# Layer 1's first convolution done in halves twice, with the projection ahead of it: two attention blocks on one core

## The chip, the cores and the metric

The kernel runs on one core of a Trainium2 chip. The metric is device time in microseconds (us), the median of three runs. A core has a tensor engine (PE; its weight loads are listed apart as PEld), VectorE (DVE), ScalarE (ACT), GpSimd (POOL), and a sync engine (SP) that mostly issues transfers (DMA). Each engine works through its own list of instructions in order; semaphores connect the lists.

## The reference, cut to what matters

Eight images of 512 channels and 32 x 32 pixels (1024 tokens) go through two attention blocks, one after the other, all in fp32:

```python
# layer 0: 32 groups, 8 heads of 64 channels
h = group_norm(x); q, k, v = split(w_qkv @ h + b_qkv)
x = x + w_proj @ (softmax(q.T k / 8) applied to v) + b_proj
# layer 1: 8 groups, one head of 512 channels
h = group_norm(x); q, k, v = q_w @ h + q_b, k_w @ h + k_b, v_w @ h + v_b
x = x + p_w @ (softmax(q.T k / sqrt(512)) applied to v) + p_b
```

All convolutions are 1 x 1, so each is a product of a 512 x 512 matrix and a 512 x 1024 image.

## The kernel before, in words

**Algebra.** In layer 1 the query and key weights are multiplied once, in a prologue, into one matrix M, and the value and output weights into Z. Layer 1 is then: g = M h (plus a bias), scores from g and h, z = Z h, and the product of the exponentials with z. So a sample has seven large stages: in layer 0 `v`, `k`, `q`, the attention of 8 heads, the projection `p`; in layer 1 `g` ("layer 1's first convolution"), the scores, `z`, the product with z.

**Halving.** Every product outside the heads is done by Winograd's form of Strassen's rule (`wino`, L227): both factors are cut in 2 x 2 blocks, sums of blocks are formed ("factors", `left_sums` L151 and `right_sums` L165), and 7 block products take the place of 8. The seven are issued in the order 1, four of `middle`, then 4 and 3; products 1, 2 share PSUM bank pair a, 6, 7, 4 pair b, 5, 3 pair c, and VectorE and ScalarE take the sums out in `done`. The last two products and what follows them are put on a list (`tail`) and issued only after the next stage's first product (`finish`), so that PE has work while the next stage's inputs become ready. `conv2` (L416) does so twice for `k` and `q`: each of the 7 products of half size is again done by 7 of quarter size, 49 matmuls of 256 columns for one convolution. For it GpSimd forms the inner factors of the image (`inner_factors`, L400: four subtractions for each of the 7 outer products), and the doubly cut weights are made once in the prologue by `keep2` (L296) and kept in DRAM.

**Order over the samples.** Layer 1 of sample b - 1 runs after the attention of sample b. One turn of the loop (L928) is: attention of sample b (eight stretches, one for each pair of heads `hp` and half of the tokens `tb`: 8 score tiles, exponentials, 8 products with v, sums, inverse); `g` of sample b - 1; projection of b; scores, z and the product with z of b - 1; `v`, `k`, `q` of b + 1. For b = 0 it is attention, `v` of sample 1, projection, `k`, `q`.

**What sets the order.** Matmuls are pinned in program order (L67). On the other engines a planner orders instructions when the kernel is built: each is placed when its inputs are expected to be ready and its buffer is free, earlier ones in the program first, so that a ready instruction may go ahead of one that stands before it; one wrapped in `tc.keep_in_program_order` ("pinned") stays behind the instruction traced just before it on its engine. Small VectorE work is queued on `background` and emitted a few pieces after each product (`run_background`), or all at once (`all_background`). `hooks` are lists of functions, one list after each product (after each pair of products in `conv2`). In attention, `extra[2 s]` is run after the scores of stretch s and `extra[2 s + 1]` after its products with v.

**Buffers.** 32 SBUF tiles of 4 KB a partition are shared by all images, factors and exponentials (`big`). Weights go through a ring of three buffers (`wpool`, 14 KB a partition each); `uses` lists the weights in order of use, and `load_weight` (L317) fetches the next one when a buffer has been read to the end. The PSUM pools are made anew for each kind of stage (`psum_pools`).

**The end of an attention stretch.** `reciprocals` (L548): PE sums the exponentials over partitions (`sums`), VectorE inverts them (L559), GpSimd keeps a running check sum (`all_recs`, L561), and the inverse goes to DRAM and back, spread over partitions (L563, L573). GpSimd then multiplies `a` (L615); in the last stretch VectorE does it later, in `scaled` (L617).

**Statistics of layer 1.** The projection's `residual` adds bias and x (L845, L847) and queues the statistics of each half (`half_stats`, L98; `end_stats`, L103) on `background`. `norm_hooks` (L861) are handed to the scores: `all_background` after the third product of the scores' first half, `group_mean` (a matmul and four small VectorE operations) after the fourth, `affine` (a matmul, then GpSimd's power) after the fifth.

**Weights for M.** The prologue's `later` prepares p, m and z during the first stretches of attention 0: three buffers of the ring, four subtractions each, a transfer to DRAM (`keep`), and after each the load of the next weight in use.

Of the kernel before, what the change touches and what calls it, by code (L numbers as in the profile page):

```python
# [29 lines left out]
def two_attention_blocks_kernel(  # L30
# [145 lines left out]
    def main_path(ctx):  # L176
# [116 lines left out]

        wdram2 = {n: dram.tile([P, 7, 7, P], F32, name=f"sums2_{n}") for n in "qk"}

        def keep2(n, t):  # L296

            u = wpool.tile([P, 4, 7, P], F32, tag="w", name=f"prepare2_{n}")
            quarter = lambda k, i: t[:, :, k, ts(i, P)]
            a11, a21, a12, a22 = quarter(0, 0), quarter(0, 1), quarter(1, 0), quarter(1, 1)  # L300
            s1, s2, s3, s4 = (u[:, i, :, :] for i in range(4))
            for dst, x, y, op in (
                (s1, a21, a22, ALU.add), (s2, s1, a11, ALU.subtract), (s3, a11, a21, ALU.subtract),
                (s4, a12, s2, ALU.subtract),
            ):
                nc.gpsimd.tensor_tensor(dst, x, y, op)
            for j, f in enumerate((a11, a12, s4, a22, s1, s2, s3)):
                nc.sync.dma_start(wdram2[n][:, :, j, :], f)

        twice = [("k", 0), ("k", 1), ("q", 0), ("q", 1)]  # L310
        uses = ["v", "p", *twice] if B > 1 else ["p"]
        for b in range(1, B):
            uses += ["m", "p", "z"] + (["v", *twice] if b + 1 < B else [])
        uses += ["m", "z"]
        loaded = []

        def load_weight():  # L317
            if uses:
                n = uses.pop(0)
                t = wpool.tile([P, 7 * C], F32, tag="w", name=f"w_{n[0]}_{len(uses)}")  # L320
                if n in twice:
                    t = t.rearrange("p (i j m) -> p i j m", i=4, j=7)
# [16 lines left out]

        def image_factors(h, uid):  # L340

            tiles = [pair_tile(f"t{i}_{uid}") for i in (1, 2, 4)]
            halves = lambda t: (t[:, :HT], t[:, HT:])
            return right_sums(
                [halves(t) for t in h[:2]], [halves(t) for t in h[2:]],
                [lambda j, t=t: t[:, j, :] for t in tiles], nc.vector.tensor_sub,
            )
# [51 lines left out]

        def inner_factors(hf, uid):  # L400

            f, steps = {}, []
            for p in ORDER:
# [5 lines left out]
                def make(ops=((t1, b12, b11), (t2, b22, t1), (t3, b22, b12), (t4, b21, t2))):  # L409
                    for dst, x, y in ops:  # L410
                        nc.gpsimd.tensor_tensor(dst, x, y, ALU.subtract)

                steps.append(make)
            return f, steps

        def conv2(n, f, bias, name, hooks=(), late=None):  # L416

# [121 lines left out]
            pair(2, (7,), [(1, 0)], [(0, 1)], [lambda: biased_half(1, 1)])  # L539
            last = [lambda: biased_half(0, 1), lambda: biased_half(1, 0)]  # L540
            if late is not None:
                late += last
                last = []
            pair(3, (3, 4), [(0, 1), (1, 0)], [(0, 1), (1, 0)], [load_weight, *last])
            return out


        def reciprocals(total, uid, across):  # L548

# [12 lines left out]
            rows = rowpool.tile([2, 4, P], F32, tag="rows", name=f"rows_{uid}")  # L562
            nc.sync.dma_start(rows.rearrange("j i n -> i j n"), rc[0:P:32, :, :])  # L563
            if across:
                r = pair_tile(f"r_{uid}")
                for j in range(2):
                    row = rows[j : j + 1].rearrange("j i n -> j (i n)")
                    nc.sync.dma_start(r[:, j, :], row.to_broadcast([P, HT]))
            else:
                r = rpool.tile([P, HT], F32, tag="r", name=f"r_{uid}")  # L570
                for j in range(2):
                    row = rows[j : j + 1].rearrange("j i n -> j (i n)")
                    nc.sync.dma_start(r[ts(j, 64), :], row.to_broadcast([64, HT]))  # L573
            return r


        def attention0(b, q, k, v, extra):
            a = channel_tiles(f"a0_{b}")
            n = 0
            for hp in range(KC):  # L580
                for tb in range(2):
                    uid = f"0_{b}_{hp}_{tb}"
# [29 lines left out]
                    nc.scalar.copy(dst, av)  # L612
                    r = reciprocals(total, uid, False)
                    if (hp, tb) != (KC - 1, 1):
                        nc.gpsimd.tensor_tensor(dst, dst, r, ALU.mult)  # L615
                    else:
                        scaled = lambda dst=dst, r=r: nc.vector.tensor_mul(dst, dst, r)  # L617

            assert not extra
            return a, scaled  # L620


        def scores1(b, gf, hf, uid, hooks):
# [7 lines left out]
            def part(j):  # L631
# [33 lines left out]

                wino(f"sc_{uid}_{j}", mm, done, middle=(6, 2, 5, 7) if j else (2, 5, 6, 7), hooks=() if j else hooks)

# [84 lines left out]
        def prologue():  # L752
# [44 lines left out]
            later = []  # L797
            for n in "pmz":
                t, steps = prepare(n)
                later.append(steps)  # L800
                later.append([lambda n=n, t=t: keep(n, t), load_weight])
            later.append([
# [3 lines left out]
            ])  # L806
            return v, q, k, norm1, later

        psum_pools("first", 2)
        v, q, k, norm0, later = prologue()  # L810

# [21 lines left out]

        def attention_steps(a, scaled, b):
            af, steps = image_factors(a, f"a_{b}")
            return af, [[], [scaled, lambda: background.extend(steps)]]

        def projection(b, af, xt):

            norm = GroupNorm(1, f"1_{b}")  # L840

            def residual(i, r, c, ps, u):
                oc = 2 * r + i
                xh = xt[oc][:, ts(c, HT)]
                nc.vector.scalar_tensor_tensor(xh, ps, obias[0][:, oc : oc + 1], xh, ALU.add, ALU.add)  # L845
                if u is not None:
                    nc.vector.tensor_add(xh, xh, u)  # L847
                background.append(lambda: norm.half_stats(oc, c, xh))

                if c == 1 - r:  # L850
                    background.append(lambda: norm.end_stats(oc))

# [4 lines left out]

            by_channel(weight("p"), af, f"p_{b}", residual, after=[load_weight, store])
            return norm

        def norm_hooks(norm, uid):  # L861
            return [
                [], [], [all_background], [lambda: norm.group_mean(acc_tile(f"gmean_{uid}")[:, :KC])],
                [lambda: norm.affine(acc_tile(f"gvar_{uid}")[:, :KC])],
            ]

        def values(b, h, hooks=()):

            hf, steps = image_factors(h, f"h0_{b}")
            background.extend(steps)  # L870
            inner, steps = inner_factors(hf, f"h0_{b}")
# [19 lines left out]

        def layer1_scores(b, h, hooks):
            hf, steps = image_factors(h, f"h1_{b}")
            background.extend(steps)
            g = conv(
                weight("m"), hf, ubias, f"g1_{b}", middle=(2, 5, 6, 7), hooks=hooks, back=4,
                after=[load_weight, lambda: background.extend(gsteps)],
            )
            stiles = [pair_tile(f"sg{i}_{b}") for i in (1, 2, 4)]
# [4 lines left out]
            )  # L904
            return hf, gf

        def layer1_rest(b, hf, gf, hooks, ahead):
            e, total, ef = scores1(b, gf, hf, f"1_{b}", hooks)
            state = {}
# [18 lines left out]
        for b in range(B):  # L928
# [11 lines left out]
            for i, f in enumerate(applies):  # L940
                extra[2 * i + 3].append(f)
            if b > 0:
                extra[0] += late
            psum_pools(f"attention_{b}", 1)
            a, scaled = attention0(b, q, k, v, extra)
            psum_pools(f"products_{b}", 2)
            xt = [load_x(b, c, "x") for c in range(KC)]
            af, ends = attention_steps(a, scaled, b)
            if b > 0:
                hf, gf = layer1_scores(b - 1, h, ends)  # L950
                norm1 = projection(b, af, xt)
                if b + 1 < B:
# [3 lines left out]
                ahead = [loads, *([f] for f in applies)]  # L956
                layer1_rest(b - 1, hf, gf, norm_hooks(norm1, f"1_{b}"), ahead)
                if b + 1 < B:
                    v, f, norm0 = values(b + 1, h)
                    q, k, late = keys_and_queries(b + 1, f, norm0, ())  # L960
            elif B > 1:
                v, f, norm0 = values(1, h, ends)
                norm1 = projection(0, af, xt)
                q, k, late = keys_and_queries(1, f, norm0, norm_hooks(norm1, "1_0")[1:])
            else:
                for f in sum(ends, []):
                    f()
                all_background()
                norm1 = projection(0, af, xt)
                finish()  # L970
                for f in sum(norm_hooks(norm1, "1_0"), []):
                    f()
                h, loads, applies = begun(load_again, norm1, 0, "h1")
                for f in loads + applies:
                    f()
        hf, gf = layer1_scores(B - 1, h, ())
        layer1_rest(B - 1, hf, gf, (), ())
        finish()

# [194 lines left out]
```

## Time and profile before

| | |
|---|---|
| time, median of 3 (lowest, highest) | 2905.97 us (2902.11, 2907.01) |
| profiled execution | 2900.9 us, granted clock 0.999 |
| one attention stretch | 14.65 us (418.17 to 432.83) |
| one turn of the loop, sample 1 to sample 2 | 355.16 us (330.10 to 685.26) |

One turn of the loop by stage, from the trace (start of the attention of sample 1 at 330.1 us):

| stage | from, to (us) | PE busy | DVE busy | POOL busy |
|---|---|---|---|---|
| `g` and most of the projection | 447.5 to 488.8 | 41.3 | 30.1 | 1.0 |
| scores and start of z | 488.8 to 537.3 | 48.5 | 27.8 | 3.2 |
| last attention stretch | 432.8 to 447.5 | 14.65 | 13.1 | 3.0 |

How to read it: busy times are the sums of the instructions' durations in the window. A matmul in fp32 is two records of the trace, each with a weight load of its own. The end of a matmul in the profile is modelled, and a record's duration overlaps with the next, so speed is read from the distance between starts. An engine that is idle while PE works costs nothing by itself. Lines in the profile name the helper (L67 for all matmuls, L238 for sums in PSUM), so stages are told apart by the names of the tiles.

### The profile page before, as it was taken

To read this page: it belongs to the slowest core of one execution; us is meant where nothing else is said; L and a number is where in the kernel's file an instruction comes from. 1 tells how busy PE (TensorE), PEld (TensorE's weight loads), DVE (VectorE), ACT (ScalarE), POOL (GpSimd) and SP (SyncE) were. 2 spreads that over 40 slices of the span, in tenths; PEclk is the share of its full clock that TensorE was granted. 3 is DMA by queue.
4 is the path that set the end of the run, shared out by engine and by line. 5 is a ranking of instruction groups with operands and counts; after the bars stand their busy time and mean duration, and the time that the engine had idled before them with its cause. 6 is when DMAs were issued, how large, how long until landed. Compare 5 with 4: busy or idle time off the path is not lost.

```text
span 2900.9 us, 29024 instructions
## 1 busy us (share of the span) xinstructions
PE 2886.5 (100%) x10838; PEld 1500.3 (52%) x10838; DVE 1932.5 (67%) x2613; ACT 872.2 (30%) x1117; POOL 468.9 (16%) x525
## 2 busy tenths in 40 slices
PE   9999999999999999999999999999999999999999
PEld 5435634565345653457434574346733458334544
DVE  5488687567766578665776557866577665776555
ACT  1251451214512055121551115411163112631110
POOL 3023210032200321003210122102121031110000
PEclk9999999999999999999999999999999999999999
DMA  8433403123122231222212232122411224011201
GB/s 277 153 137 109 159 19 110 72 103 132 34 98 92 95 113 48 84 92 105 107 48 80 92 135 77 48 80 99 154 55 44 80 103 151 26 59 65 94 1 66
DMA packets 84186, 267.97 MB, mean 92 GB/s; under 512 B 10371, under 2 KB 29891, under 8 KB 75974
## 3 DMA queue, kind: packets, MB, share of 16 engines
q1 hardware_dynamic: 83622, 265.89, 25.5%
q8 instruction: 87, 1.43, 0.2%
q14 instruction: 61, 0.50, 0.1%
q10 hardware_dynamic: 416, 0.16, 0.0%
HBM read 216.30 MB, written 49.72 MB: 92 GB/s over the span
## 4 chain that ended last, share of the span: by engine, by line
PE 98%; issue 1%; DVE 0%; POOL 0%; ACT 0%; DVEq 0%; POOLq 0%
PE sc L67 16%; PE av L67 15%; PE psb_sc L67 6%; PE psb_av L67 6%; PE psa_av L67 4%; PE psa_sc L67 4%; PE psc_av L67 4%; PE psc_sc L67 4%; PE psb_g L67 3%; PE psb_z L67 3%; PE psb_p L67 3%; PE psb_v L67 3%; PE psb_k L67 3%; PE psb_q L67 2%; PE psa_g L67 2%; PE psa_v L67 2%
## 5 line engine op out<-in xcount | busy, mean ns | idle before, releaser
L598 DVE TENSOR_TENSOR sum<-sum,e 128x1024 f32<-128x1024 f32 x384 | 518.6, 1351 | 40.4 <-DVE sum L598 0.5
L594 ACT ACTIVATE e<-sc 128x1024 f32<-128x1024 f32 x512 | 476.8, 1052 | 72.9 <-PE sc L67 72.9
L67 PE MATMUL sc<-q,k 64*128 64x512 f32 x2048 | 458.3, 596 | 0.0
L67 PE MATMUL av<-e,v 128*64 128x512 f32 x2048 | 453.6, 595 | 0.0
L67 PEld LDWEIGHTS sc<-q,k 64*128 64x128 f32 x2048 | 192.3, 186 | 239.3 <-ACT e L594 110.3
L67 PEld LDWEIGHTS av<-e,v 128*64 128x64 f32 x2048 | 141.4, 137 | 304.3 <-issue 302.3
L561 POOL TENSOR_TENSOR all_recs<-all_recs,rc 128x256 f32<-128x256 f32 x72 | 64.4, 894 | 880.2 <-DVE rc L559 880.2
L559 DVE RECIPROCAL rc<-sums 128x256 f32<-128x256 f32 x72 | 126.4, 1756 | 89.7 <-PE sums L67 87.4
L615 POOL TENSOR_TENSOR a<-a,r 128x512 f32<-128x512 f32 x56 | 109.5, 1955 | 274.0 <-DMA r<-rows 247.5
L646 ACT ACTIVATE e<-e 128x512 f32<-128x512 f32 x96 | 60.5, 630 | 232.7 <-DVE e L645 232.7
L612 ACT COPY a<-av 128x512 f32<-128x512 f32 x64 | 37.4, 585 | 305.2 <-PE av L67 305.2
L596 DVE TENSOR_TENSOR sum<-e,e 128x1024 f32<-128x1024 f32 x64 | 78.6, 1228 | 59.8 <-ACT e L594 59.8
L67 PE MATMUL psa_sc<-g,h 128*128 128x512 f32 x256 | 115.7, 594 | 0.0
L67 PE MATMUL psa_av<-e,z 128*128 128x512 f32 x256 | 113.3, 595 | 0.0
L128 POOL TENSOR_TENSOR rstd<-ve,mhalf 128x4 f32<-128x4 f32 x16 | 16.7, 1043 | 499.9 <-DVE ve L126 499.9
L140 ACT ACTIVATE h<-h,b,s 128x1024 f32<-128x1024 f32 x62 | 78.5, 1270 | 60.7 <-DMA h<-in_x 48.0
L67 PEld LDWEIGHTS psa_sc<-g,h 128*128 128x128 f32 x256 | 48.1, 190 | 57.9 <-issue 56.2
L67 PEld LDWEIGHTS psa_av<-e,z 128*128 128x128 f32 x256 | 48.0, 190 | 57.3 <-issue 55.4
L67 PE MATMUL psb_k<-inner_h,w_k 128*128 128x256 f32 x294 | 75.4, 383 | 0.0
L67 PE MATMUL psb_q<-inner_h,w_q 128*128 128x256 f32 x294 | 74.9, 383 | 0.0
L249 ACT COPY t_sc<-psa_sc 128x512 f32<-128x512 f32 x32 | 18.7, 585 | 181.7 <-DVE x L847 152.4
L444 POOL TENSOR_TENSOR k<-k,k 128x256 f32<-128x256 f32 x28 | 20.0, 727 | 291.0 <-DVE u_k L439 291.0
(304 smaller groups left out, 4580.8 us busy)
## 6 DMA issues: line engine op xcount, KB each, us to landing
x<-in_x SPq DMA_DIRECT2D x36, 512.0 KB
h<-in_x SPq DMA_DIRECT2D x32, 512.0 KB
r<-rows SPq DMA_DIRECT2D x128, 128.0 KB
spill<-x SPq DMA_DIRECT2D x32, 512.0 KB
h<-spill SPq DMA_DIRECT2D x32, 512.0 KB
x<-spill SPq DMA_DIRECT2D x32, 512.0 KB
out<-x SPq DMA_DIRECT2D x64, 256.0 KB
w_p<-sums_p SPq DMA_DIRECT2D x8, 1792.0 KB
```

Of the source, the lines that this page charges most:

```text
L67: tc.keep_in_program_order(nc.tensor.matmul(*args, **kw))
L140: tc.keep_in_program_order(nc.scalar.activation(dst, src, AF.Identity, bias=b, scale=s))
L249: nc.scalar.copy(t1[i], ps["a", i])
L444: nc.gpsimd.tensor_tensor(d, x, y, ALU.add)
L559: nc.vector.reciprocal(rc, sums)
L561: nc.gpsimd.tensor_tensor(all_recs, all_recs, rc, ALU.add)
L594: nc.scalar.activation(e, sc, AF.Exp, scale=(C // 8) ** -0.5)
L596: nc.vector.tensor_add(total, es[0], e)
L598: nc.vector.tensor_add(total, total, e)
L612: nc.scalar.copy(dst, av)
L615: nc.gpsimd.tensor_tensor(dst, dst, r, ALU.mult)
L646: nc.scalar.activation(dst, dst, AF.Exp, scale=scale)
```

## The change

Seven of the eight convolutions `g` (all but the last sample's, which has no projection beside it) are done by `conv2`, in halves twice. To have the image's inner factors ready, the order of stages is turned: after the attention of sample b first the projection of b, then `g` of b - 1; GpSimd forms the inner factors of layer 1's h behind its last addition of the attention, beside the projection. As the projection now follows attention at once, its factors of `a` and those of layer 1's h are made during attention, about two subtractions a stretch (pinned for `a`); the last stretches are taken in the order (3, 1), (3, 0), so that only the last factor of `a` waits for the very last stretch, and that stretch's inverse goes through ScalarE's queue (`queue`). The projection's products run in the order 1, 5, 6, 7, 2, 4, 3. Its statistics no longer run beside it: they are gathered in `stats`, put in the background after the third product of the scores' first half, emptied after the second product of the second half, and the group's mean and variance follow the third and fourth product there. `layer1_rest` begins with `finish()`, so `g`'s last products and biases come before the scores' first product. `keep2` for M runs once, after attention 0 (`more_later`), in a buffer of the ring; `p`'s first load comes after it. The rest of the diff hands functions and lists around.

```diff
-        wdram2 = {n: dram.tile([P, 7, 7, P], F32, name=f"sums2_{n}") for n in "qk"}
+        wdram2 = {n: dram.tile([P, 7, 7, P], F32, name=f"sums2_{n}") for n in "qkm"}
...
-                nc.gpsimd.tensor_tensor(dst, x, y, op)
+                tc.keep_in_program_order(nc.gpsimd.tensor_tensor(dst, x, y, op))
...
         for b in range(1, B):
-            uses += ["m", "p", "z"] + (["v", *twice] if b + 1 < B else [])
+            uses += ["p", *twice["m"], "z"] + (["v", *twice["k"], *twice["q"]] if b + 1 < B else [])
         uses += ["m", "z"]
...
-        def inner_factors(hf, uid):
+        def inner_factors(hf, uid, pin=lambda ins: ins):
...
-                        nc.gpsimd.tensor_tensor(dst, x, y, ALU.subtract)
+                        pin(nc.gpsimd.tensor_tensor(dst, x, y, ALU.subtract))
...
-            last = [lambda: biased_half(0, 1), lambda: biased_half(1, 0)]
+            last = [lambda: biased_half(1, 0), lambda: biased_half(0, 1)]
...
-                for tb in range(2):
+                for tb in (0, 1) if hp < KC - 1 else (1, 0):
...
-                    r = reciprocals(total, uid, False)
-                    if (hp, tb) != (KC - 1, 1):
+
+                    last = (hp, tb) == (KC - 1, 0)
+                    r = reciprocals(total, uid, False, nc.scalar if last else nc.sync)
+                    if not last:
                         nc.gpsimd.tensor_tensor(dst, dst, r, ALU.mult)
                     else:
-                        scaled = lambda dst=dst, r=r: nc.vector.tensor_mul(dst, dst, r)
+                        scaled = lambda dst=dst, r=r: tc.keep_in_program_order(nc.vector.tensor_mul(dst, dst, r))
...
-            for n in "pmz":
+            for n in "pzm":
                 t, steps = prepare(n)
                 later.append(steps)
-                later.append([lambda n=n, t=t: keep(n, t), load_weight])
+                later.append([lambda n=n, t=t: keep(n, t)])
+            later[1].append(load_weight)
...
-            return v, q, k, norm1, later
+            return v, q, k, norm1, later, lambda: (keep2("m", t), load_weight())
...
-                background.append(lambda: norm.half_stats(oc, c, xh))
+                stats.append(lambda: norm.half_stats(oc, c, xh))
 
                 if c == 1 - r:
-                    background.append(lambda: norm.end_stats(oc))
+                    stats.append(lambda: norm.end_stats(oc))
...
-            by_channel(weight("p"), af, f"p_{b}", residual, after=[load_weight, store])
-            return norm
+            by_channel(
+                weight("p"), af, f"p_{b}", residual, middle=(5, 6, 7, 2), hooks=[[], [], hooks, [], [add_rest]],
+                after=[load_weight, store],
+            )
+            return norm, stats
 
         def norm_hooks(norm, uid):
+
             return [
-                [], [], [all_background], [lambda: norm.group_mean(acc_tile(f"gmean_{uid}")[:, :KC])],
+                [], [all_background], [lambda: norm.group_mean(acc_tile(f"gmean_{uid}")[:, :KC])],
                 [lambda: norm.affine(acc_tile(f"gvar_{uid}")[:, :KC])],
             ]
...
+            if inner:
+                g = conv2("m", inner, ubias, f"g1_{b}", after=after)
+            else:
+                g = conv(weight("m"), hf, ubias, f"g1_{b}", middle=(2, 5, 6, 7), back=4, after=[load_weight, *after])
...
         def layer1_rest(b, hf, gf, hooks, ahead):
+
+            finish()
             e, total, ef = scores1(b, gf, hf, f"1_{b}", hooks)
...
             for i, f in enumerate(applies):
-                extra[2 * i + 3].append(f)
+                extra[2 * i + 1].append(f)
...
             if b > 0:
+                hf, t = image_factors(h, f"h1_{b - 1}")
                 extra[0] += late
+                for i, fs in enumerate((t[:1], t[1:2], (t[2], t[4]), (t[6], t[3]), (t[5], t[7]), steps[:2], steps[2:4])):
+                    extra[2 * i + 3] += fs
...
             if b > 0:
-                hf, gf = layer1_scores(b - 1, h, ends)
-                norm1 = projection(b, af, xt)
+
+                inner, sums2 = inner_factors(hf, f"h1_{b - 1}", tc.keep_in_program_order)
+                for f in sums2:
+                    f()
+                norm1, stats = projection(b, af, xt, [scaled, steps[7]])
+                gf = layer1_scores(b - 1, hf, inner)
...
+                hooks = [[], [], [lambda: background.extend(stats)]], norm_hooks(norm1, f"1_{b}")
+                layer1_rest(b - 1, hf, gf, hooks, ahead)
...
             elif B > 1:
-                v, f, norm0 = values(1, h, ends)
-                norm1 = projection(0, af, xt)
-                q, k, late = keys_and_queries(1, f, norm0, norm_hooks(norm1, "1_0")[1:])
+                more_later()
+                v, f, norm0 = values(1, hf, [[], steps[:4], steps[4:7], [scaled, steps[7]]])
+                norm1, stats = projection(0, af, xt)
+                load_weight()
+                hooks = norm_hooks(norm1, "1_0")
+                hooks[0].append(lambda: background.extend(stats))
+                q, k, late = keys_and_queries(1, f, norm0, hooks)
```

## Prediction

> **What bounds the kernel now.** I read the busy times first, then the waits of the tensor engine, then its timeline, since a busy share says nothing of speed.
>
> ```profile
> PE 2886.5 (100%) x10838; PEld 1500.3 (52%) x10838; DVE 1932.5 (67%) x2613; ACT 872.2 (30%) x1117; POOL 468.9 (16%) x525
> PE 98%; issue 1%; DVE 0%; POOL 0%; ACT 0%; DVEq 0%; POOLq 0%
> ```
>
> PE is busy in 2886.5 of 2900.9 us and is 98% of the chain that ended last. Two lines of the list of what PE waited for:
>
> ```profile
> PE tr_wk L70 <- DMA rawk<-in_w: 4.0, 2, 3.8
> ...
> PE psc_q L67 <- DVE c_q L439: 0.4, 1, 0.4
> ```
>
> All seven lines of it add up to under 8 us, nearly all in the prologue. So time moves in two ways only: fewer PE columns, or new gaps in PE. The timeline of PE gives the price of a column (start, duration, count):
>
> ```profile
> 454.45 3.60 PE L67 MATMUL psc_g<-t_h,w_m 128*128 128x512 f32 x8
> 457.89 3.60 PE L67 MATMUL psb_g<-t_h,w_m 128*128 128x512 f32 x8
> ...
> 647.43 1.89 PE L67 MATMUL psb_k<-inner_h,w_k 128*128 128x256 f32 x8
> 649.16 0.59 PE L67 MATMUL psa_k<-h,w_k 128*128 128x256 f32 x2
> ```
>
> Starts, not durations, are to be read: eight 512-column records take 457.89 - 454.45 = 3.44 us, 429 ns each (finer over many records: 429.2); eight 256-column ones 1.73 us, 216 ns each (215.9). Halving the columns halves the time.
>
> [...] the mean durations, 592 and 379 ns, would make a convolution done twice dearer (98 x 379 = 37.1 us against 56 x 592 = 33.2); the spacings say the reverse. [...] GpSimd's multiplication of `a` took 1.27 us at 150.16 and 2.08 at 440.25, among VectorE's sums. [...] The trace shows no single landing; its fullest stretch moved 305 GB/s, and I use 270 GB/s, what it moved while weights and images were loaded together (310 to 320 us: 268).
>
> **The change, part by part.**
>
> *Layer 1's first convolution, seven samples of eight.* Before: 7 products x 2 x 2 matmuls of two records, 56 records x 429.2 = 24.04 us. After: 7 x 7 matmuls, 98 records x 215.9 = 21.16. That saves 2.88 us each, 20.2 in all. A doubled convolution has small waits of its own. `k` in sample 2 starts at 634.44 and ends at 663.75, with 6.95 us of `v` and 0.86 of `q` in between: 21.50 us, 0.34 over the sum. Taken for the new one too: 7 x 0.34 = 2.4 lost. VectorE and ScalarE have room: in 447 to 489 us VectorE was busy 30.1 of 41.3, and 8 of its operations (h's factors) and 4 of a's leave this stage.
>
> *Products of h for it on GpSimd.* 28 subtractions, which took 22.8 us at 590 to 612.8 beside VectorE. They start once the last sums are inverted, some 3 us after attention, and are done by 26 us. The convolution now comes 17.2 us after attention's end (five products of the projection), its second pair of products some 12 us later; the first pair needs 8 of them, 6 us. Hidden by the projection.
>
> *Projection first.* Its first four products (1, 5, 6, 7: 13.7 us) need nothing of the last attention stretch. Product 2 needs the scaled `a`: in the stretch before, the inverse is ready at 434.78 and the multiplication starts at 440.25, 5.5 us. Sums at 447.5, inverse at 449.3, so scaled by 456, against 461.2. Queued on ScalarE the transfers hold that engine some 3 us, to 452.3, and behind them are the two copies of product 1, done by 453.5 and wanted by the sums of product 6 at 447.5 + 8.6 = 456.1. The residual's x: loads were issued at 437.75 and the transfers' share falls to 3% after 447; wanted from 461 on. Nothing is exposed, even if fewer free buffers put them 5 us later.
>
> *Order of the last biases.* After the convolution's last matmul: two VectorE additions (0.81 us), one ScalarE bias (0.72) and hand-over, about 2.1 us, under the 3.4 us of the scores' first product. Hidden.
>
> *Factors in attention.* Two VectorE subtractions a stretch, 1.29 us:
>
> ```profile
> 422.71 8.75 DVE L598 TENSOR_TENSOR sum<-sum,e 128x1024 f32<-128x1024 f32 x6
> 433.02 1.76 DVE L559 RECIPROCAL rc<-sums 128x256 f32<-128x256 f32 x1 [1.56 <-PE sums L67]
> ```
>
> VectorE idles 1.56 us between sums and inverse; put there, they fit. h's subtractions are not pinned; the trace shows that the planner moves such ones (L170 of `t_h` at 445.99, ahead of an inverse that precedes it in the program). Ahead of the sums they find only 0.74 us of idle (434.81 + 0.42 to 435.98) and 0.8 us between the sums' end (431.46) and PE's use (432.26). I take the place behind the sums, since h is ready only in the middle of a stretch: 0; bound 0.5 us a stretch.
>
> *Statistics in the scores.* 8 statistics of 0.61 us and 4 aggregations of 0.12, 5.4 us, move to the scores' first half; the group mean moves from 17 us after the scores' start to 34, the variance to 38. In between everything left in the background goes to VectorE at once, ahead of the mean's copy. What stands there now:
>
> ```profile
> 529.24 1.29 DVE L171 TENSOR_TENSOR t<-e,t 128x512 f32<-128x512 f32 x2
> 535.78 0.69 DVE L238 TENSOR_TENSOR w_sc<-psb_sc,t_sc 128x512 f32<-128x512 f32 x1 [5.26 <-PE psb_sc L67]
> ```
>
> VectorE is full from 518.6 to 530.5 and then idle 5.26 us. The variance's matmul would come at 534 on this clock. Added: 2.9 us of statistics and 1.2 of subtractions that now come at 538.8; the mean's small chain is 0.75. So it is ready between 530.5 + 2.9 + 0.75 = 534.2 and 535.4, if the planner leaves those subtractions behind or not, and up to 536 with a little idling: 0 to 2 us a sample. I take 0.
>
> *The doubled weights of M, once.* GpSimd's four operations on 896 columns:
>
> ```profile
> 51.71 8.32 POOL L306 TENSOR_TENSOR prepare_q<-prepare_q 128x896 f32<-128x896 f32 x4 [25.29 <-DMA x<-in_x]
> ...
> 254.84 3.60 PE L67 MATMUL psa_p<-a,w_p 128*128 128x512 f32 x8
> ```
>
> The same four for M are pinned behind attention 0's last GpSimd addition, some 3.5 us after 237.5, so 241 to 249.3, or 252 if VectorE gets between. The weights are a ring of three buffers: `p` can be loaded only when M's prepared tile has been read, so from 249.3. With the last part of M's sums before it, 0.46 + 1.79 MB at 270 GB/s are 8.3 us, and 2 us for start and completion (my guess from the 5.5 us that two small transfers in a row took above): 259.6 to 262.5. Before, `p` was loaded at 155.5. The projection's first product comes at 254.84 and would wait 4.8 to 7.7 us; without the last part ahead of it and at 305 GB/s 2.5, with the next image's 2 MB in the way 13. Queued behind it on PE is everything. I take 7, once. In later samples three weight buffers are still loaded ahead: when `p` ends `z` is fetched, and both halves of M lie there since the end of `q`: 0.
>
> Sum: -20.2 + 2.4 + 7 = -10.8 us; 2905.97 - 10.8 = 2895.2.
>
> **Rivals.**
> - *All hidden* (`p` comes in time): -17.8, 2888. For it: the transfer engines are at 17% in 250 to 260 us. Against: the ring of three.
> - *The mean waits behind the background*: 2 us in 7 samples, 14 more: 2909. For it: VectorE full for 12 us just there. Against: the 5.26 us of idle behind it.
> - *Sums late in attention*: the subtractions go ahead of the sums; 0.5 us in 5 stretches of 7 samples and 4 of the first, 19.5 more: 2914.7, slower than before. For it: unpinned, and 0.8 us of slack. Against: 1.56 us of idle behind the sums. More tiles live at once (three factors of h, two of a) could add to this by holding up exponentials.
>
> **Chances.** Forecast 0.50, all hidden 0.15, mean waits 0.15, sums late 0.20. The range leaves out the last and what lies under the full 20.2: 2886 to 2914. The bound of 0.2% is 5.8 us, so faster ends at 2900.2. Forecast: 0.43 of its 0.50 are below this, 0.07 (a longer wait for `p`) within. All hidden: faster. Mean waits: 0.12 within, 0.03 over. Sums late: slower. Faster 0.58, same 0.19, slower 0.23.
>
> **What would show it.** `g` as 98 records a sample with 216 ns spacing, and 56 of 429 in the last. A gap of some 7 us in PE before `psa_p` near 255 us and none like it later. The time from attention's end to the scores' start shorter by some 2.5 us. PE's waits on VectorE at the group's variance near zero; if not, the second rival. Stretches of attention still 14.65 us apart; if not, the third. Wrong altogether if the scaled `a` comes later than 13.7 us after attention, or if a doubled convolution with biases on the path waits much longer than `k` did.

## The result

The changed kernel takes 2921.73 us (median of 4 runs, 2920.43 to 2922.45) against 2904.07 for the kernel before on the same chip: a ratio of 1.0059, 95% interval 1.0042 to 1.0077. It is 17.7 us slower; the forecast was 2895.2, and its range ended at 2914.

The profile's first lines after, busy times and the chain that ended last:

```profile
PE 2879.2 (99%) x11132; PEld 1556.1 (53%) x11132; DVE 1999.1 (68%) x2753; ACT 923.1 (32%) x1201; POOL 685.1 (23%) x781
...
PE 12%; DVE 1%; issue 0%; ACT 0%; DVEq 0%
```

PE is busy for 7 us less than before, in a span 18.4 us longer. The chain covers only some 13% of the span, so it is no help here. What PE waited for (total, times, longest):

```profile
PE psa_p L67 <- DMA w_p<-sums_p: 10.7, 1, 10.7
PE psc_v L67 <- DVE v L375: 6.6, 1, 6.6
...
PE gmean L67 <- DVE mv L103: 3.8, 7, 0.5
PE sums L67 <- DVE sum L598: 1.6, 3, 1.0
PE psb_k L67 <- DVE u_k L439: 1.4, 2, 1.1
```

Five lines that were not there. The first two happen once, `gmean` seven times. I call a **turn** the time from the start of one attention to the start of the next. Read from PE's timeline, the first turn went from 209.80 to 235.74 us (+25.9), the six others from 2131.4 to 2125.3 together (-6.0), the end from 439.5 to 438.5 (-1.0), the prologue by -0.5: 18.4 in all, the difference of the two spans. Between versions I compare turns: each version has a single profiled execution, and the prologues alone differ by up to 2.4 us. A turn's doubled convolution ought to bring 2.88 us; a typical turn went from 355.16 to 354.23, which is 0.93. So there are two questions: what broke the first turn, and where two thirds of the gain of the others are.

**The first turn.** PE's timeline of the changed kernel, start and duration:

```profile
252.61 3.62 PE L67 MATMUL psb_v<-w_v,h 128*128 128x256 f32 x16
266.95 5.69 PE L67 MATMUL psa_p<-a,w_p 128*128 128x512 f32 x8 [10.72 <-DMA w_p<-sums_p]
272.48 3.62 PE L67 MATMUL psb_v<-w_v,t_h 128*128 128x256 f32 x16
282.66 6.38 PE L67 MATMUL psc_v<-w_v,h 128*128 128x256 f32 x16 [6.57 <-DVE v L375]
288.88 3.60 PE L67 MATMUL psc_p<-t_a,w_p 128*128 128x512 f32 x8
```

There are two gaps, and after each gap the work itself is slow: the product at 266.95 takes 272.48 - 266.95 = 5.53 us where such a product takes 3.43, the one at 282.66 takes 6.22 instead of 3.45. The table by stretch gives the granted clock (the last number but two of a line):

```profile
core 0: us, PE busy (x) PEld busy (x) DVE busy (x) ACT busy (x) POOL busy (x), PEclk, DMA share, GB/s
255.00:262.00 7.00, 1.23 (x6) 0.74 (x4) 0.68 (x2) 0.00 (x0) 7.00 (x9) 0.91 0.59 174
262.00:270.00 8.00, 3.05 (x4) 1.52 (x5) 1.89 (x4) 0.00 (x0) 3.22 (x5) 0.50 0.99 413
```

It is 0.50 from 262 to 270 us, and again from 281.3 to 288.1, behind the second gap. Why `p` was late is on GpSimd:

```profile
231.85 1.68 POOL L617 TENSOR_TENSOR a<-a,r 128x512 f32<-128x512 f32 x1 [4.82 <-ACT e L594]
233.49 1.71 POOL L411 TENSOR_TENSOR inner_h<-h 128x256 f32<-128x256 f32 x1
...
247.58 0.72 POOL L561 TENSOR_TENSOR all_recs<-all_recs,rc 128x256 f32<-128x256 f32 x1
248.26 8.76 POOL L306 TENSOR_TENSOR prepare_m<-prepare_m 128x896 f32<-128x896 f32 x4
```

and on the queue of SyncE:

```profile
258.32 1.12 SPq L328 DMA_DIRECT2D w_p<-sums_p  x1
```

Sixteen of the inner factors of `h` for sample 1, which have no fixed place, were put ahead of attention 0's last addition, so M's doubling begins at 248.26 and not at 241. `p` is asked for at 258.32 and used from 266.95. The second gap is VectorE's. The loads of the next sample's image stand behind `p` in the same queue, and VectorE stands, in order, before their statistics:

```profile
255.00 0.68 DVE L238 TENSOR_TENSOR w_v<-psb_v,t_v 128x512 f32<-128x512 f32 x1
268.11 1.29 DVE L98 BATCH_NORM_STATS2 bnst<-ahead 128x6 f32<-128x512 f32 x2 [12.43 <-DMA ahead<-in_x]
269.31 0.68 DVE L238 TENSOR_TENSOR w_v<-psb_v,t_v 128x512 f32<-128x512 f32 x1
...
281.92 1.28 DVE L375 TENSOR_TENSOR v<-psc_v,w_v 128x512 f32<-128x512 f32 x2
```

VectorE stands still for 12.43 us and then has statistics and factors of `a` to do, almost without a pause (it waits once, 1.94 us), before the sum that frees v's buffer at 281.92. So this gap hangs on the image's loads and on what VectorE's list holds ahead of that sum; that `p` is late does not by itself make it (the second experiment shortens the first gap and not this one).

**A later turn.** In sample 1's turn the doubled convolution has 98 records, 216 ns apart but for six small waits: 21.88 us for the 21.16 of its columns, 0.72 more. The scores' first two products take 7.07 us for 6.87. In the attention one last sum is held back, because VectorE had factors placed ahead of it:

```profile
418.83 7.43 DVE L598 TENSOR_TENSOR sum<-sum,e 128x1024 f32<-128x1024 f32 x5
426.18 1.29 DVE L173 TENSOR_TENSOR t_h<-h,t_h 128x512 f32<-128x512 f32 x2
427.38 1.22 DVE L598 TENSOR_TENSOR sum<-sum,e 128x1024 f32<-128x1024 f32 x1
```

Attention takes 117.66 instead of 117.45. And PE waits for the mean:

```profile
550.30 3.60 PE L67 MATMUL psa_sc<-g,h 128*128 128x512 f32 x8
554.45 0.39 PE L67 MATMUL gmean<-mv,gm 128*128 128x4 f32 x2 [0.55 <-DVE mv L103]
554.69 3.68 PE L67 MATMUL psc_sc<-sg,t_h 128*128 128x512 f32 x8
```

554.45 - 550.30 is 4.15 us instead of 3.43, and `gmean` 0.24 instead of 0.14: 0.82. Altogether 0.72 + 0.20 + 0.21 + 0.82 = 1.95, and 2.88 - 1.95 = 0.93, what was measured.

### The profile page after: what moved, and what is told of

Same layout as the page of the kernel before. It is cut to its first block, busy times and chain, and to the rows that moved or that the text cites. A ratio compares the mean times of both kernels' runs of the same rounds, so it can differ in the third digit from the quotient of the medians.

```text
span 2919.3 us, 30267 instructions
## 1 busy us (share of the span) xinstructions
PE 2879.2 (99%) x11132; PEld 1556.1 (53%) x11132; DVE 1999.1 (68%) x2753; ACT 923.1 (32%) x1201; POOL 685.1 (23%) x781
## 5 line engine op out<-in xcount | busy, mean ns | idle before, releaser
L411 POOL TENSOR_TENSOR inner_h<-h,inner_h 128x256 f32<-128x256 f32 x112 | 95.6, 856 | 2.7
L411 POOL TENSOR_TENSOR inner_h<-h 128x256 f32<-128x256 f32 x56 | 57.0, 1018 | 151.3 <-PE psc_av L67 151.3
L652 POOL COPY sum<-e 128x1024 f32<-128x1024 f32 x8 | 12.5, 1557 | 283.6 <-ACT e L648 283.6
```

The lines of the kernel that those rows point to most:

```text
L411: pin(nc.gpsimd.tensor_tensor(dst, x, y, ALU.subtract))
```

## The experiments

My theory was that the loss is all in the first turn's order of work: three engines that work their queues in order, one late transfer, and a slow clock behind each gap. The rivals were that the transfer alone matters, or that the new work itself is too much for VectorE, whatever its order.

**M's doubling earlier.** The call that doubles M and asks for `p` goes from the end of attention 0 into its fifth stretch:

```
+                extra[9].append(more_later)
...
-                more_later()
```

> The changed kernel with the doubled weights of M made, and p fetched, in the middle of attention 0 (after its fifth stretch) and not behind it. Theory A (the loss is the once-only wait in sample 1's v and projection, 25.9 us of the 17 lost): attention 0's start to attention 1's start falls from 235.7 us to 211 to 214, no wait of the projection for p, none of v's last product for VectorE, total 2897 to 2901. Rival B (a wait of the same size appears elsewhere: GpSimd's four long operations hold VectorE's sums in attention): the stretch behind them is longer by 4 to 8 us and the total stays above 2905. Rival C (the turns are slow, the once-only wait is a side effect): total above 2915.

2917.4 us, ratio 1.0042 (1.0029 to 1.0056); first turn 231.45. The gap before `p` is gone, and another has come in the middle of attention 0. PE's timeline:

```profile
202.48 1.08 PE L67 MATMUL sums<-sum,ones 128*32 128x256 f32 x8 [8.76 <-DVE sum L598]
203.50 9.56 PE L67 MATMUL sc<-q,k 64*128 64x512 f32 x32
```

The sums come 8.76 us late. GpSimd's timeline ahead of that:

```profile
190.32 11.03 POOL L306 TENSOR_TENSOR prepare_m<-prepare_m 128x896 f32<-128x896 f32 x4
```

and VectorE's in the same time:

```profile
194.39 5.03 DVE L171 TENSOR_TENSOR t_h<-h,t_h 128x512 f32<-128x512 f32 x2
199.34 3.08 DVE L598 TENSOR_TENSOR sum<-sum,e 128x1024 f32<-128x1024 f32 x1
```

While GpSimd works, two subtractions of VectorE take 5.03 us instead of 1.29. The rival was right about this place. A second wait, of 4.89 us, came in `v`, where a's factors stood on VectorE beside GpSimd's inner factors. The total also lies above the 2915 of the rival of slow turns, but the later turns are about 354.3 us, as in the changed kernel: what is lost is lost in the first turn.

**The inner factors behind M's doubling.** The 28 inner factors of sample 1 get a fixed place in program order, which is after M's doubling:

```
-            inner, steps = inner_factors(hf, f"h0_{b}")
+            inner, steps = inner_factors(hf, f"h0_{b}", tc.keep_in_program_order if b == 1 else lambda ins: ins)
```

> The changed kernel with one thing more: the inner factors of sample 1's h for v, k and q are pinned behind the doubling of M's weights on GpSimd. In the trace of the changed kernel 16 of them ran ahead and the doubling began at 248.3 in place of 241. If the planner's hoisting is what made the wait for p 10.7 us, the doubling begins at 241 to 242, p is asked for some 7 us earlier, the wait falls to 2 to 4 us, and the total to 2908 to 2914. Rival (the transfer itself, not its start, is late): the wait stays over 8 us and the total over 2918.

2914.4 us, ratio 1.0038 (1.0024 to 1.0051); first turn 227.43. M's doubling began at 242.36, `p` was asked for at 251.97, and the gap before it fell from 10.72 to 3.62 us. So the sixteen instructions ahead were the cause of that part. The second gap grew from 6.57 to 8.44, and with it the total stayed just above the 2908 to 2914 I had expected: VectorE still stood before the image's statistics (5.77 us), and still had them and the factors of `a` ahead of v's sum.

**The clock.** Products whose results nobody reads fill both gaps, twelve (24 records) before the projection and seven before v's last product:

```
+                dummy(12)
+                tail.insert(1, lambda: dummy(7))
                 norm1, stats = projection(0, af, xt)
```

> The changed kernel with 12 matmuls of 512 columns that nothing reads, put where the projection waits for p, and 7 more where v's last product waits for VectorE: the same waits, but PE is busy in them. It computes the same outputs. If PE is slower for a while after an idle gap (records of 850 and not 429 ns after it), those records are back at 429 ns and the total falls by 4 to 5 us, to 2917. If the slow records have another cause (the data's arrival), they stay and the total is 2921 to 2923 or more.

2916.52 us, ratio 1.004 (1.0024 to 1.0055); first turn 230.95, 4.8 us less than in the changed kernel, although work was added:

```profile
269.52 3.67 PE L67 MATMUL psa_p<-a,w_p 128*128 128x512 f32 x8 [0.46 <-DMA w_p<-sums_p]
...
282.92 3.72 PE L67 MATMUL psc_v<-w_v,h 128*128 128x256 f32 x16 [0.26 <-DVE v L375]
```

From the start of attention 0 on, `p` comes no earlier than in the changed kernel (147.35 us against 147.17), but the two products take 3.5 us each again, and the granted clock is 1.00 from 262 to 270 us. The slow clock cost 2.1 + 2.8 = 4.9 us, and PE's standing idle brought it, not the transfers, which go on beside PE here too. In the changed kernel's trace the gaps are 10.7 and 6.6 us, with a clock of 0.50 behind both, for 4.1 and 5.4 us of the work. The gaps of the other runs are in the last section.

**The statistics later.** In the first turn the next image's loads and statistics go from `v` to the keys (the rest of the edit keeps the later turns as they were):

```
-                    background.append(lambda c=c: norm.stats(c, load_x(b + 1, c, "ahead")))
...
+                    late_stats.extend(ahead)
...
-                hooks[0].append(lambda: background.extend(stats))
+                hooks[0].append(lambda: background.extend(late_stats + stats))
```

> The changed kernel with the statistics of sample 2's x (and their loads) moved from sample 1's v to the keys behind the projection. If the second wait (6.6 us, v's last product for VectorE) comes from VectorE standing in order behind statistics whose loads queue behind p, it goes, with the slow records behind it: 7 to 9 us less, 2912 to 2915. Rival (VectorE is simply full after the first wait): it stays above 3 us and the total falls by under 3 us.

2928.88 us, ratio 1.0081 (1.0066 to 1.0097); first turn 242.26. I had expected a gain. The waits of PE:

```profile
PE psa_p L67 <- DMA w_p<-sums_p: 14.4, 1, 14.4
PE psb_k L67 <- DVE k L439: 6.2, 1, 6.2
...
PE psb_k L67 <- DVE u_k L439: 3.2, 1, 3.2
```

The gap at `v` is gone, as expected. But a's factors now ran on VectorE from 242.8 on, against GpSimd's inner factors, which took 1.17 us each instead of 0.72; counted from the start of attention 0, M's doubling began 3.2 us later and the projection 3.7. And in the keys VectorE stood before the same statistics. So the one wait went, the one before it grew, and two others came.

**The order mended.** Three edits together: M's doubling by VectorE, one operation after the sums in each of four stretches of attention 0, and then `p`; a's factors of sample 0 behind the middle products of `v`; h's factors in the attentions in program order, behind the sums (shown for the first attention).

```
+            engine = nc.vector if n == "m" else nc.gpsimd
...
+                hf, t = image_factors(h, "h0_1", lambda *t: tc.keep_in_program_order(nc.vector.tensor_sub(*t)))
...
+                    extra[(6, 8, 10, 12, 13, 13)[i]].append(f)
...
-                v, f, norm0 = values(1, hf, [[], steps[:4], steps[4:7], [scaled, steps[7]]])
+                v, f, norm0 = values(1, hf, [[], [], [], [], steps[:4], steps[4:6], [scaled, *steps[6:]]])
```

> The program with the order of the first turn mended: M's second round of factors made by VectorE, one operation in each of four stretches of the first attention, and p asked for from there; the factors of the attention's output for sample 0 moved behind the products of v that need VectorE; in every attention the factors of h kept behind the sums. Theory A (the loss is three waits of the first turn, each with a slow clock behind it, and nothing later loses): first turn about 211 us, no wait of over 1.5 us at p's first product, at v's or in the first attention, later turns about 354.1, total about 2896 us. Rival B (four more operations of 1 us on a VectorE that already has eleven us of sums in each stretch make sums late[...]): a wait at the sums of two or more us in stretches 3 to 6 and a first turn of 217 or more, total over 2902.

2897.13 us, ratio 0.9973 (0.9963 to 0.9982), some 25 us below the changed kernel. First turn 212.58, later ones 354.04. PE's waits at the same places:

```profile
PE gmean L67 <- DVE mv L103: 3.9, 7, 0.6
PE psb_k L67 <- DVE u_k L448: 1.1, 1, 1.1
...
PE sums L67 <- DVE sum L607: 0.4, 1, 0.4
```

Both gaps are gone, and VectorE has room for M:

```profile
224.17 1.08 DVE L304 TENSOR_TENSOR prepare_m<-prepare_m 128x896 f32<-128x896 f32 x1
```

**The price of the doubling.** The mended order, with layer 1's first convolution done with one halving in the same place (GpSimd's inner factors of `h` for it go too):

```
-                gf = layer1_scores(b - 1, hf, inner)
+                gf = layer1_scores(b - 1, hf, None)
```

> As the mended order, but layer 1's first convolution done with one halving in the seven turns (98 short products again 56 long ones, no inner factors of h), in the same place behind p. It prices the doubling alone. If a turn's doubling is worth its arithmetic less the waits seen in the trace, 2.88 less about 0.75 us, this kernel is 7 x 2.1 = 15 us longer than the mended order, with turns of 356.2. Rival: if moving the convolution behind p, not the doubling, cost the missing part of a turn's saving (only 0.93 of 2.88 arrived), then this kernel's turns exceed 356.5, longer than the kernel before's 355.16.

2911.07 us, ratio 1.0021 (1.0011 to 1.003): 13.9 us more than with the doubling. A turn is 356.05, 2.02 longer. So doubling is worth 2.0 us a turn, not the 2.88 of its columns, and the 0.93 that arrived was this less what the new order costs. Against the kernel before (355.16) the order alone, without doubling, costs 0.9 a turn, and nearly all of that lies in the scores, where PE waits for `gmean`'s input (4.5 us in seven turns).

**The mean one step later.** The mended order, with an empty step ahead of the group mean in the scores of those samples, so that mean and variance each come one product later:

```
+                hooks = [[], [], [lambda: background.extend(stats)]], [first, others[0], [], *others[1:]]
```

> As the mended order, but in layer 1's scores the product for the group means and the one for their variances each stand one step later in TensorE's order. If the 0.8 us a sample in front of the means' product are only its place ahead of VectorE's aggregation, they go: turns 353.3 to 353.6 and a total 4 to 5 us below the mended order. Rival: VectorE falls behind in this stage altogether (it has statistics, sums and factors there), so the wait moves to the variances' product or to the next products that need its factors, and the total changes by less than 1.5 us.

2891.49 us, ratio 0.9956 (0.9942 to 0.997), 5.6 below the mended order and 0.4% below the kernel before: the best version. Turns are 353.22, the 0.82 us of each is gone, and no wait at `gmean` is left:

```profile
531.78 3.60 PE L67 MATMUL psc_sc<-sg,t_h 128*128 128x512 f32 x8
535.22 0.28 PE L67 MATMUL gmean<-mv,gm 128*128 128x4 f32 x2
535.36 3.68 PE L67 MATMUL psb_sc<-g,h 128*128 128x512 f32 x8
538.87 0.28 PE L67 MATMUL gvar<-dv,gm 128*128 128x4 f32 x2
```

**Only M's doubling on VectorE.** The mended order without its other two edits.

> Of the mended order only the doubling of M by VectorE and the earlier request for p. [...] p's wait goes and the sums are on time; v's sums stay late, for the factors of the attention's output still alternate with GpSimd's inner factors of h on VectorE: a wait of 3 to 5 us at v's second product of the middle and a first turn of 216 to 220, total 2903 to 2907. Rival: if the inner factors alone, with M out of the way, run early enough, the first turn is 211 to 213 and the two other edits are worth nothing, total about 2897.

2911.27 us, ratio 1.0022 (1.0013 to 1.0032); first turn 225.46, later ones 354.24. `p` came in time, and `v` waited 8.18 us, at the factors of `a`. I had said 3 to 5, and a total of 2903 to 2907. The move of a's factors was not tried alone; this run, which lacks it, has its longest wait there. VectorE's timeline:

```profile
246.97 1.29 DVE L98 BATCH_NORM_STATS2 bnst<-ahead 128x6 f32<-128x512 f32 x2 [3.02 <-DMA ahead<-in_x]
253.62 0.69 DVE L238 TENSOR_TENSOR u_v<-psb_v,t_v 128x512 f32<-128x512 f32 x1 [5.36 <-PE psb_v L67]
...
254.34 8.95 DVE L966 TENSOR_TENSOR t_a<-a 128x512 f32<-128x512 f32 x2
```

The two subtractions at 254.34 are what `v` waits for. GpSimd's stream beside them, two of its lines:

```profile
254.08 0.72 POOL L420 TENSOR_TENSOR inner_h<-h 128x256 f32<-128x256 f32 x1
254.76 0.72 POOL L420 TENSOR_TENSOR inner_h<-h,h 128x256 f32<-128x256 f32 x1
```

GpSimd goes on at 0.72 us each, twelve of them from 254.08 to 262.73. The two subtractions of VectorE take 8.95 us for 1.29 and end at 263.29, 0.56 behind the last of the twelve. The sum with one input in PSUM, 0.72 us earlier, took its usual 0.69, and the statistics, with a single input, their usual 1.29, in the middle of GpSimd's work.

**M's doubling on GpSimd, but spread out.** The best version, with the four operations on GpSimd in the same four stretches:

```
-            engine = nc.vector if n == "m" else nc.gpsimd
+            engine = nc.gpsimd
```

> As the version with the means a step later, but M's second round of factors on GpSimd again, one operation in each of four stretches of the first attention instead of four in a row. Theory A (the harm is GpSimd's work back to back[...]): a single operation of 2 to 3 us holds VectorE once, the idle time behind the sums takes most of it up, waits for sums of at most 1 us in up to four stretches, total 0 to 4 us over that version. Rival B (any GpSimd operation of that length ahead of the sums makes them late): waits of 1.5 to 2 us in each of the four stretches, some with a slow clock behind them, total 6 to 12 us over.

2896.07 us, ratio 0.9972 (0.996 to 0.9983); first turn 217.65 against 212.50 in the best version, 5.15 more, with later turns the same. The sums waited:

```profile
196.11 0.64 PE L67 MATMUL sums<-sum,ones 128*32 128x256 f32 x8 [3.00 <-DVE sum L607]
212.87 0.64 PE L67 MATMUL sums<-sum,ones 128*32 128x256 f32 x8 [0.34 <-DVE sum L607]
228.43 0.64 PE L67 MATMUL sums<-sum,ones 128*32 128x256 f32 x8 [0.83 <-DVE sum L607]
```

This lies between the two expectations: one wait of 3 us and two small ones. Behind the wait of 3.00 us the clock fell, with PE already back at work:

```profile
196.10:197.26 1.16, 1.15 (x12) 0.51 (x14) 1.16 (x3) 0.00 (x0) 0.00 (x0) 1.00 0.32 100
197.26:200.67 3.41, 3.41 (x12) 1.37 (x10) 2.09 (x2) 1.72 (x2) 0.90 (x1) 0.50 0.00 1
```

That cost another 1.7 us. Single operations hurt too, 5.15 us in all, though less than four in a row, with one wait of 8.76 us and 2.9 of slow clock behind it.

**h's factors without a fixed place.** The best version, with those subtractions free for the planner to place.

> As the version with the means a step later, but the factors of h in the attentions again without a fixed place. If the planner's placing of them ahead of a last sum costs the 0.2 us an attention that the timeline of the changed kernel shows, this is 8 x 0.2 = 1.6 us longer, turns of 353.4 instead of 353.2, first attention up to 2 us longer. Rival: with VectorE's operations of M among them, the free placing does as well, no difference over 0.5 us.

2893.97 us, ratio 0.9965 (0.9951 to 0.9978). Turns are 353.42 instead of 353.22, attention 117.67 instead of 117.46, the first turn is 214.28 instead of 212.50, all of it in attention 0 (119.93 instead of 118.15), and the end is 0.5 longer: 3.5 us in all (1.8 + 6 x 0.2 + 0.5). The medians differ by 2.5; this run's prologue was 1.5 us shorter. That is what I had expected for a planner that places them badly.

## Why the prediction was wrong

Term by term, in us, forecast and then what the changed kernel's trace shows:

| term | forecast | measured |
|---|---|---|
| fewer columns, 7 x 2.88 | -20.2 | -20.2 |
| own waits of the doubled convolution | +2.4 | 7 x 0.72 = +5.0 |
| `p` late, once | +7 | +10.7 |
| v's second wait, once | none | +6.6 |
| slow clock behind the two gaps | none | +4.9 |
| attention 0, and the keys after it | 0 | 1.7 + 1.8 = +3.5 |
| mean in the scores | 0 | 7 x 0.82 = +5.7 |
| scores' first two products | 0 | 7 x 0.20 = +1.4 |
| factors in attention | 0 | 7 x 0.21 = +1.5 |
| sum | -10.8 | +19.1 |

The first row is counted, records by spacing. The spans differ by 18.4; a prologue 0.5 us shorter and small differences between turns are the rest.

The part that failed most is the first turn: priced as one wait of 7 us, it lost 25.9. The later turns and the end were to bring 17.8 and brought 7.1.

- **The saving** was right: 98 records 216 ns apart, 56 of 429 in the last sample.
- **`p` late.** The mechanism was right, the place near 255 us too; the size was off, and lay inside its bounds of 2.5 to 13. The step that failed is "pinned behind attention 0's last GpSimd addition, some 3.5 us after 237.5". I followed the instruction ahead in program order and forgot that unpinned ones can be put ahead of that: the doubling began at 248.26. With the inner factors put behind, the wait was 3.62.
- **"Queued behind it on PE is everything."** This was the largest error: 6.6 us, and 2.8 of slow clock behind them. I named PE's queue alone. Behind `p` in the transfers' queue were the image's loads, behind these on VectorE the statistics, and behind those v's sums, for which PE waits again. The statement of nothing like it later was wrong by that.
- **The clock** had no term. The work behind the two gaps ran at a granted clock of 0.50 for 4.1 and 5.4 us: 4.9 us lost, shown by the filled gaps.
- **The mean.** I took 0 of 0 to 2 us a sample; it is 0.82. The view was nearly right (VectorE is busy for 10.86 of the 11.9 us that I called full), but I expected the variance to be late, and it was the mean: its product waits for the statistics, among which the planner had put sums. The rival with 2 us was too dear.
- **Factors in attention.** I took 0 of 0 to 0.5 us a stretch. The planner put them ahead of a last sum in one stretch of eight: 0.21 an attention. In attention 0 they are the likely cause of its 1.7 us: two stand ahead of a last sum at 175.31, and the last experiment, with the same free placing, lost 1.8 there. So the rival of late sums did happen, at 3.2 us and not at its 19.5.
- **Own waits.** 0.34, from `k`, was 0.72: `g` has a bias and its last waits come just ahead of the scores. I did not try which of the six waits the bias makes.
- **Hidden parts.** The scaled `a`, the loads of x and GpSimd's inner products of `h` in the later turns were hidden, as said: with the order mended those turns show no wait for them. The last biases are hidden, if the 0.2 us at the scores' start isn't theirs, which I did not try.

The mended order with the mean later comes to 2891.5, close to the forecast. That does not make the forecast right: it was made for a first turn that the change did not have, and the two agree by luck. The keys of the first turn are 1.8 us longer even there. In the trace VectorE makes the projection's statistics among k's sums, from 292.93 to 303.04, where the kernel before had them done at 290.0; that this makes the keys' waits is read and not tried.

## What to carry to other kernels

Where a change puts a transfer or an operation into a place that is crossed once, follow everything that stands behind it in every queue, not the bounding engine's alone, and count what the planner may still put ahead of it. Look at the granted clock behind each gap in PE that a change brings: behind eight gaps of 3.00 to 14.4 us here, work at 0.50 cost another 1.5 to 3.1 us, behind one of 3.62 us nothing. An instruction of GpSimd among VectorE's sums isn't free even when GpSimd is idle: price it by what VectorE has due. M's four operations on GpSimd, one in each of four stretches, made the sums wait 3.00, 0.34 and 0.83 us.

## What the runs showed of the hardware

- The granted clock was 0.50 behind eight gaps in PE. Each gap, and what the slow clock cost: 10.72 us (2.1) and 6.57 (2.8) in the changed kernel, 8.76 (2.9) and 4.89 (3.1) with M's doubling earlier, 8.44 (1.5) with the inner factors behind M's doubling, 14.4 (2.7) with the statistics later, 8.18 (2.8) with only M's doubling on VectorE, 3.00 (1.7) with it spread out on GpSimd. So it cost no more behind a longer gap. Behind one of 3.62 us (the inner factors behind M's doubling) the clock was 1.00: the length alone does not decide, and what does was not shown. In the changed kernel the clock was 0.50 for 10.24 and 6.83 us and fell 6.2 and 1.4 us before PE was back at work; with M's doubling spread out on GpSimd it was 0.50 for 3.41 us and fell 1.2 us after.
- Two subtractions of VectorE with both inputs in SBUF, 1.29 us elsewhere, took 8.95 us beside twelve GpSimd instructions of 0.72 us each (only M's doubling on VectorE). Beside a stream of the same instructions in another run (the later statistics) two of them took 2.34 us, and GpSimd's 1.17 each. What decides between the two no run here shows. In the first of these streams VectorE's sum with one input in PSUM took 0.69 us, and two statistics, with a single input, 1.29 us, as elsewhere.
- 128 x 896 with two inputs took VectorE 1.08 us in the mended order. GpSimd took 2.08 for the same in the prologue (four in 8.32 us), and up to 3.07 among VectorE's sums with M's doubling spread out.
